# Layer 0 of a four-layer convolution kernel: its transfers divided anew among three queues, Wu in column tiles, an image's opening emitted in parts

## The chip, the cores and the metric

The kernel runs on one core of a Trainium2 chip. A core has TensorE (PE: matmuls; PEld is its loading of weights), VectorE (DVE), ScalarE (ACT), GpSimd (POOL) and SyncE (SP); transfers are issued from the queues of SP, ACT and POOL. The metric is device time in microseconds (us) of one execution, the median of several. The program is written with a tile layer that decides from the emitted code in which order each engine meets its instructions and where it waits.[...]

## The reference

The input is x with shape (32, 8, 256, 256) in float32. There are four layers, each x = x + f(groupnorm(x)); the change touches layer 0 alone.

```python
def _L0_conv_ref(x, K_local, Wp, bp, Wu, bu, Wg1, bg1, Wg2, bg2):
    R, EPS, BETA, STEPS = (3.9, 0.3, 0.15, 15)
    drive = x
    grid = drive
    for _ in range(STEPS):                                  # "the lattice"
        mapped = R * grid * (1.0 - grid)
        local = _conv(mapped, K_local, groups=8)            # 3x3, depthwise
        physics = (1.0 - EPS) * mapped + EPS * local
        grid = (1.0 - BETA) * physics + BETA * drive
    cml_out = jnp.clip(grid, 0.0001, 1.0 - 0.0001)
    h = jax.nn.relu(_conv(x, Wp, bp))                       # 3x3, 8 -> 128 channels
    nca_out = jax.nn.sigmoid(_conv(h, Wu, bu))              # 1x1, 128 -> 8
    gin = jnp.concatenate([x, cml_out, nca_out], axis=1)    # 24 channels
    g = jax.nn.sigmoid(_conv(jax.nn.relu(_conv(gin, Wg1, bg1)), Wg2, bg2))
    return g * cml_out + (1.0 - g) * nca_out

x = x + _L0_conv_ref(_gn(x), ...)    # _gn: 4 groups of 2 channels, mean and variance of each image
x = x + _L1_conv_ref(_gn(x), ...)    # quantised 3x3 convolution
x = x + _L2_conv_ref(_gn(x), ...)    # 3x3 convolution
x = x + _L3_conv_ref(_gn(x), ...)    # 5x5 depthwise convolution
```

## The kernel before

For each image two generators are interleaved: `lattice(b)` (load, sums, normalisation, 15 steps, result to DRAM) and `gated(b - 1)` (the hidden layer with Wp and Wu, then the gate). Each `yield` of the lattice says how much of its image is emitted, and the driver emits as much gated work beside it. The lattice of image b needs its own earlier steps; the gated work of image b - 1 needs only what lies in DRAM.

```python
def spread(half):                       # border points of neighbouring patches, 4 transfers
    ...
        nc.sync.dma_start(to[q : q + n * m, 0:long], window(state, at, dims))

def lattice(b):
    xi = xb[:, :, 1 : 1 + W]            # xb: one buffer for all images
    nc.gpsimd.dma_start(xi, x[b].rearrange("c (k r) w -> (c k) r w", k=HB))
    nc.gpsimd.dma_start(on_rows(xr_d[b % 3], W), x[b].rearrange(...))
    bn = small.tile([P, RB, 6], F32, name="bn0")
    for r in range(RB):
        nc.vector.bn_stats(bn[:, r, :], xb[:, r, 1 : 1 + W])
    group_stats(psum, bn, st, gavg_sb)  # two tiny matmuls (L94, L101), a square root on ACT
    yield 3
    ...                                 # flat (dr) and xb: normalised, on DVE
    nc.gpsimd.dma_start(window(xn_d[b % 3], ...), xb.rearrange("p r w -> p (r w)"))
    nc.gpsimd.dma_start(on_rows(nr_d[b % 3], WP), xb)
    yield 3
    for t4 in range(TX // 4):           # 32 transposes (L259), copied back by ACT
        ...
        if t4 % 4 == 3:
            yield 0.5
    for c in range(C):                  # first state, on DVE; spread after channels 3 and 7
        ...
    yield 1
    for step in range(STEPS):
        for half in range(2):           # "half-step": four channels
            for c in range(4 * half, 4 * half + 4):
                ps = ps_c.tile([P, 512], F32, name="psc")
                nc.tensor.matmul(o, patch_sb[:, c, :], v, start=True, stop=False)       # L281
                nc.tensor.matmul(o, ring_sb[:, c, :], rings[half]..., start=False, stop=True)  # L282
                nc.vector.scalar_tensor_tensor(v, o, FLOOR, dr[:, c], ALU.max, ALU.add)
                nc.vector.scalar_tensor_tensor(v, v, 1.0, v, ALU.subtract, ALU.mult)    # not in the last step
            spread(half)                # not in the last step
            yield 1
    for t4 in range(TX // 4):           # 32 transposes back (L302), copied to xb by DVE
        ...
    nc.gpsimd.dma_start(on_rows(cr_d[b % 3], WP), xb)

def gated(b):
    beside(nc.gpsimd, ha, nr, 0)        # rows beside each block, for the whole image
    beside(nc.gpsimd, ha, cr, 48)
    def hidden(r2):                     # two rows of every block, 16 rows of positions
        pn = ps_n.tile([P, 512], F32, name="psn")
        def second(hh, r):              # Wu in a 128-column weight, all columns but 8 zero
            nc.tensor.matmul(
                pn, wu_sb[:, C * (RB - 1 - r) : C * (RB - 1 - r) + P], hh,              # L344
                start=r == 0, stop=r == RB - 1,
            )
        for half in range(2):
            im = imp.tile([72, 2, 8 * WP], F32, name="im")      # two buffers
            ...nc.scalar.dma_start(im[...], window(xn, ...))    # 6 transfers
            for j in range(8):
                nc.tensor.matmul(ph, wp_sb, im[:, :, j * WP : j * WP + W], ...)         # L360
                nc.scalar.activation(hh, ph, AF.Relu, bias=bp_sb)
                if late is not None:
                    second(*late)
                late = (hh, 8 * half + j)
                yield
        second(*late)
        nc.scalar.activation(nh[:, 2 * r2 : 2 * r2 + 2, 1 : 1 + W], pn..., AF.Sigmoid, bias=bu_sb)
        beside_two(r2)                  # hb, from nh, on SP
    def gate(r2):
        ...                             # xq, cq, xc loaded on ACT
        for s, src in enumerate((xq, cq, nh[:, k0 : k0 + 2, :])):
            for dx in range(3):
                nc.tensor.matmul(o, wg1_sb[:, s, dx, :], src[:, :, dx : dx + W], ...)   # L393
            yield
        nc.tensor.matmul(o, wga_sb, ha[:, k0 : k0 + 2, 0:W], start=False, stop=False)   # L398
        nc.tensor.matmul(o, wgb_sb, hb[:, k0 : k0 + 2, 0:W], start=False, stop=True)    # L399
        nc.scalar.activation(g1, pg, AF.Relu, bias=bg1_sb)
        yield
        nc.tensor.matmul(pq, wg2_sb, g1, start=True, stop=True)                         # L404
        nc.scalar.activation(gt, pq, AF.Sigmoid, bias=bg2_sb)
        nc.gpsimd.tensor_tensor(df, ci, ni, ALU.subtract)
        nc.gpsimd.tensor_tensor(gt, gt, df, ALU.mult)
        nc.vector.tensor_tensor(gt, gt, ni, ALU.add)                                    # L413
        nc.vector.tensor_tensor(xc, xc, gt, ALU.add)                                    # L414
        ...                             # sums and extremes on DVE
        nc.gpsimd.dma_start(x1_d[b][:, bass.ts(r2, 512)], flat)
        yield
    for r2 in range(NCH + 1):           # NCH = 8
        if r2 < NCH:
            yield from hidden(r2)
        if r2 > 0:
            yield from gate(r2 - 1)

for b in range(B):
    at = 0
    for load in lattice(b):
        at += load
        due = ((b - 1.2) * LATTICE + at) * GATED / LATTICE
        while done < due:
            next(rest); done += 1
```

## Time and profile before

| | |
|---|---|
| time, median of 3 runs | 21,496.32 us (21,488.26 to 21,503.26) |
| span of the profiled execution | 21,491.9 us |
| mean granted TensorE clock | 0.948 |
| layer 0 (to its last Wu matmul) | 18,904 us |
| DVE busy | 38% |
| ACT busy | 19% |
| POOL busy | 7% |
| transfers | 2,307.92 MB, mean 107 GB/s |

How to read it: busy shares are averages over the whole span; where work waits is read from the timeline and from the stretches around one image. A row of a group gives line, engine, operation, tiles out<-in, shapes and count, then busy time in us, mean ns of one, and the engine's idle time before it with what ended it. Ends of matmuls are modelled, so their rate is read from start to start. The granted clock is the share of full speed at which TensorE was allowed to run.

### The profile page before, as it was taken

The page shows a single profiled execution, that of the slowest core. Times are in us where ns is not written, and L with a number is a line of the kernel's source. Part 1 is how long each engine was busy: PE and PEld are TensorE (multiplying, and loading weights), DVE is VectorE, ACT ScalarE, POOL GpSimd, SP SyncE. Part 2 cuts the span into 40 slices and gives each one's busy share as a digit, 9 for nine tenths or more (in the row PEclk, how much of TensorE's full clock was granted, in tenths as well). Part 3 has the DMA queues.
Part 4 walks back from the last instruction along what each step waited for, and adds up shares of the span by engine and source line. Part 5 has one row for each costly group of instructions (what it writes and reads, how often), then busy time and mean ns, then how long its engine had stood idle before and what let it go on. Part 6 is the DMA issues. An engine that isn't in the chain of part 4 may idle for free.

```text
span 21491.9 us, 137690 instructions
## 1 busy us (share of the span) xinstructions
PE 19778.0 (92%) x46664; PEld 8662.7 (40%) x46664; DVE 8103.2 (38%) x13657; ACT 4075.8 (19%) x5790; POOL 1570.3 (7%) x1649
## 2 busy tenths in 40 slices
PE   6899999999999999999999999999999999989999
PEld 2343443434343444444343434344443434434444
DVE  4333333333333333333333333333333333245554
ACT  0111222212212111222222212121122222211110
POOL 0000000000000000000000000000000000011111
PEclk8999999999999999999999999999999999999999
DMA  5444444444444444444444444444444444345554
GB/s 112 104 104 105 103 109 106 107 108 108 105 109 106 108 103 106 105 105 108 105 110 107 107 106 108 107 106 102 105 106 108 107 107 105 84 106 126 126 126 109
DMA packets 525150, 2307.92 MB, mean 107 GB/s; under 512 B 111468, under 2 KB 179540, under 8 KB 356388
## 3 DMA queue, kind: packets, MB, share of 16 engines
q1 hardware_dynamic: 213668, 835.31, 21.3%
q10 hardware_dynamic: 172032, 810.61, 13.3%
q0 software_dynamic: 138752, 653.18, 11.5%
q8 instruction: 377, 6.18, 0.1%
q14 instruction: 321, 2.63, 0.0%
HBM read 1129.33 MB, written 471.38 MB: 74 GB/s over the span
## 4 chain that ended last, share of the span: by engine, by line
PE 79%; issue 8%; DMA 7%; DVE 3%; POOL 1%; ACT 1%; SPq 0%; ACTq 0%; POOLq 0%; DVEq 0%
PE ph L360 15%; PE psn L344 15%; PE psc L282 14%; PE psc L281 14%; PE pg L393 7%; PE psv L578 5%; PE psv L499 4%; DMA rings<-state 2%; DMA hb<-nh 2%; DMA xb<-in_x 1%; PE psv L503 1%; PE pq L404 1%; PE psv L582 1%; PE pg L399 1%; PE pg L398 1%
## 5 line engine op out<-in xcount | busy, mean ns | idle before, releaser
L289 DVE SCALAR_TENSOR_TENSOR state<-psc,dr 128x512 f32<-128x512 f32 x3840 | 2620.8, 689 | 7462.1 <-PE psc L282 5203.8
L365 ACT ACTIVATE hh<-ph,bp_sb 128x512 f32<-128x512 f32 x4096 | 2812.6, 687 | 8527.0 <-PE ph L360 7196.7
L360 PE MATMUL ph<-im,wp_sb 72*128 72x512 f32 x8192 | 4301.8, 622 | 26.6 <-DMA im<-xn_d 14.1
L282 PE MATMUL psc<-rings,ring_sb 80*128 80x512 f32 x7680 | 4006.9, 607 | 325.5 <-issue 271.6
L344 PE MATMUL psn<-hh,wu_sb 128*128 128x512 f32 x8192 | 4255.1, 612 | 21.8 <-ACT hh L365 21.7
L281 PE MATMUL psc<-state,patch_sb 128*128 128x512 f32 x7680 | 3932.0, 597 | 117.5 <-DVE state L289 115.5
L360 PEld LDWEIGHTS ph<-im,wp_sb 72*128 72x128 f32 x8192 | 1614.7, 199 | 2063.1 <-issue 1449.1
L344 PEld LDWEIGHTS psn<-hh,wu_sb 128*128 128x128 f32 x8192 | 1565.4, 194 | 2182.1 <-issue 1841.7
L291 DVE SCALAR_TENSOR_TENSOR state<-state 128x512 f32<-128x512 f32 x3584 | 2387.4, 695 | 30.5
L282 PEld LDWEIGHTS psc<-rings,ring_sb 80*128 80x128 f32 x7680 | 1478.6, 194 | 2215.4 <-issue 2194.8
L281 PEld LDWEIGHTS psc<-state,patch_sb 128*128 128x128 f32 x7680 | 1448.5, 190 | 2047.9 <-issue 1696.9
L413 DVE TENSOR_TENSOR gt<-gt,nh 128x512 f32<-128x512 f32 x256 | 177.9, 695 | 3176.7 <-POOL gt L412 3176.7
L412 POOL TENSOR_TENSOR gt<-gt,df 128x512 f32<-128x512 f32 x256 | 328.9, 1285 | 12404.6 <-ACT gt L406 11178.1
L578 PE MATMUL psv<-xr,w_sb 128*128 128x512 f32 x2560 | 1159.9, 595 | 0.5 <-DVE xr L563 0.5
L401 ACT ACTIVATE g<-pg,bg_sb 128x512 f32<-128x512 f32 x256 | 176.3, 689 | 3642.6 <-PE pg L399 3185.5
L94 PE MATMUL ps<-mv,gavg_sb 128*128 128x1 f32 x64 | 17.8, 348 | 785.1 <-DVE mv L92 785.1
L393 PE MATMUL pg<-xq,wg_sb 128*128 128x512 f32 x1536 | 713.4, 596 | 0.0
L499 PE MATMUL psv<-xh,w_sb 128*128 128x512 f32 x1536 | 704.1, 595 | 8.1 <-DVE xh L535 4.1
L578 PEld LDWEIGHTS psv<-xr,w_sb 128*128 128x128 f32 x2560 | 475.5, 189 | 565.5 <-issue 561.1
L393 PE MATMUL pg<-nh,wg_sb 128*128 128x512 f32 x1536 | 701.2, 592 | 0.0
L393 PE MATMUL pg<-cq,wg_sb 128*128 128x512 f32 x1536 | 701.0, 592 | 0.0
L411 POOL TENSOR_TENSOR df<-cq,nh 128x512 f32<-128x512 f32 x256 | 436.6, 1706 | 2127.7 <-ACT nh L371 2021.2
(132 smaller groups left out, 9430.8 us busy)
## 6 DMA issues: line engine op xcount, KB each, us to landing
im<-xn_d ACTq DMA_DIRECT2D x3072, 193.3 KB
rings<-state SPq DMA_DIRECT2D x1920, 213.8 KB
rings<-state SPq DMA_DIRECT2D x1920, 142.5 KB
xn_d<-xb POOLq DMA_DIRECT2D x32, 2064.0 KB, 23.6
nr_d<-xb POOLq DMA_DIRECT2D x32, 2064.0 KB, 29.4
xq<-nr_d ACTq DMA_DIRECT2D x128, 516.0 KB
cr_d<-xb POOLq DMA_DIRECT2D x32, 2064.0 KB, 11.2
cq<-cr_d ACTq DMA_DIRECT2D x128, 516.0 KB
```

Of the source, the lines that this page charges most:

```text
L281: nc.tensor.matmul(o, patch_sb[:, c, :], v, start=True, stop=False)
L282: nc.tensor.matmul(o, ring_sb[:, c, :], rings[half][:, c % 4, 0 : TX * SY].rearrange("p (x y) -> p x y", y=SY)[:, :, 0:TY], start=False, s ...
L289: nc.vector.scalar_tensor_tensor(v, o, FLOOR, dr[:, c], ALU.max, ALU.add)
L291: nc.vector.scalar_tensor_tensor(v, v, 1.0, v, ALU.subtract, ALU.mult)
L344: nc.tensor.matmul(pn, wu_sb[:, C * (RB - 1 - r) : C * (RB - 1 - r) + P], hh, start=r == 0, stop=r == RB - 1,)
L360: nc.tensor.matmul(ph.rearrange("p (k w) -> p k w", w=W), wp_sb, im[:, :, j * WP : j * WP + W], start=True, stop=True,)
L365: nc.scalar.activation(hh, ph, AF.Relu, bias=bp_sb)
L393: nc.tensor.matmul(o, wg1_sb[:, s, dx, :], src[:, :, dx : dx + W], start=s == dx == 0, stop=False,)
L411: nc.gpsimd.tensor_tensor(df, ci, ni, ALU.subtract)
L412: nc.gpsimd.tensor_tensor(gt, gt, df, ALU.mult)
L499: nc.tensor.matmul(o, w[:, dx, :], src[:, 2 * i : 2 * i + 2, dx : dx + W], start=dx == 0, stop=False,)
L578: nc.tensor.matmul(o, w3_sb[:, dx, :], xr[:, k, 2 * g : 2 * g + 2, dx : dx + W], start=dx == 0, stop=False,)
```

## The change

It touches the emission and placement of layer 0, not what it computes.

- Transfers: an image's own large ones (xb, xr_d, xn_d, nr_d, cr_d) go from POOL's queue to SP's; the im loads from ACT's to POOL's; the rows beside a block (ha, hb) from POOL's and SP's to ACT's, per quarter of an image or per pair of blocks and in two buffers instead of one whole-image buffer.
- Wu: a weight of 32 columns that writes a quarter of the partitions of pn, with rows ordered so that successive matmuls alternate between two such quarters, four at a time.
- An image's load, sums and normalisation: a `yield` after the load, so that gated work is emitted between load and sums, and other weights for the later parts.
- The gate: one pair of blocks later than before, emitted within the hidden layer of a later pair.
- Two products of the gate go from POOL to DVE; pg takes its bank from another pool.

```diff
-            nc.gpsimd.dma_start(xi, x[b].rearrange("c (k r) w -> (c k) r w", k=HB))
-            nc.gpsimd.dma_start(
+            nc.sync.dma_start(xi, x[b].rearrange("c (k r) w -> (c k) r w", k=HB))
+            nc.sync.dma_start(
                 on_rows(xr_d[b % 3], W), x[b].rearrange("c (k r) w -> (c k) r w", k=HB)
             )
+            yield 6
...
             group_stats(psum, bn, st, gavg_sb)
-            yield 3
+            yield 2
...
-            nc.gpsimd.dma_start(
+            nc.sync.dma_start(
                 window(xn_d[b % 3], WP, [[HP * WP, C], [RB * WP, HB], [1, RB * WP]]),
                 xb.rearrange("p r w -> p (r w)"),
             )
-            nc.gpsimd.dma_start(on_rows(nr_d[b % 3], WP), xb)
+            nc.sync.dma_start(on_rows(nr_d[b % 3], WP), xb)
             yield 3
...
-            yield 1
+            yield 1.5
...
-            nc.gpsimd.dma_start(on_rows(cr_d[b % 3], WP), xb)
+            nc.sync.dma_start(on_rows(cr_d[b % 3], WP), xb)
...
-                def second(hh, r):
-                    nc.tensor.matmul(
-                        pn, wu_sb[:, C * (RB - 1 - r) : C * (RB - 1 - r) + P], hh,
-                        start=r == 0, stop=r == RB - 1,
-                    )
+                def second():
+                    for hh, r in late:
+                        q, i = divmod(r, 4)
+                        nc.tensor.matmul(
+                            pn[32 * q : 32 * q + 32, :], wu_sb[:, i, :], hh,
+                            start=i == 0, stop=i == 3,
+                        )
+                    late.clear()
...
-                            nc.scalar.dma_start(
+                            nc.gpsimd.dma_start(
                                 im[24 * dy : 24 * dy + 24, k, 0:run],
...
-                    for j in range(8):
...
+                    for rows in ((0, 4, 1, 5), (2, 6, 3, 7)):
+                        four = []
+                        for i, j in enumerate(rows):
...
+                            hh = hp.tile([P, 512], F32, name="hh", bufs=6)
+                            nc.scalar.activation(hh, ph, AF.Relu, bias=bp_sb)
+                            four.append((hh, 8 * half + j))
+                            if i == 1:
+                                second()
+                            yield
+                        late += four
+                second()
...
-                beside_two(r2)
+                if r2 > 0:
+                    beside_blocks(hbs[(r2 - 1) % 2], nh, 0, 2 * r2 - 2, 2, 1)
+                if r2 == NCH - 1:
+                    beside_blocks(hbs[r2 % 2], nh, 0, 2 * r2, 2, 1)
...
+                    quarter["ha"] = qp.tile([96, 4, WP], F32, name="ha")
+                    for q, t in ((0, nr), (48, cr)):
+                        beside_blocks(quarter["ha"], t, q, k0, 4, 0)      # on ACT's queue
...
-                pg = psum.tile([P, 512], F32, name="pg", tag="ps")
+                pg = ps_n.tile([P, 512], F32, name="pg", tag="pn")
...
-                nc.gpsimd.tensor_tensor(df, ci, ni, ALU.subtract)
-                nc.gpsimd.tensor_tensor(gt, gt, df, ALU.mult)
+                nc.vector.tensor_tensor(df, ci, ni, ALU.subtract)
+                nc.vector.tensor_tensor(gt, gt, df, ALU.mult)
...
-            for r2 in range(NCH + 1):
-                if r2 < NCH:
-                    yield from hidden(r2)
-                if r2 > 0:
-                    yield from gate(r2 - 1)
+            gates = (None for r2 in range(NCH) for _ in gate(r2))
+            for r2 in range(NCH):
+                for i, _ in enumerate(hidden(r2)):
+                    yield
+                    if r2 > 1 and i % 3 == 2:
+                        next(gates)
+                        yield
+            for _ in gates:
+                yield
...
-                due = ((b - 1.2) * LATTICE + at) * GATED / LATTICE
+                due = ((b - 1.25) * LATTICE + at) * GATED / LATTICE
...
-    wu = np.zeros((P, 2 * P - C), f)
-    wu[:, P - C : P] = inputs["L0_conv_Wu"][:, :, 0, 0].T
+    wu = np.zeros((P, 4, 4, C), f)
+    for r in range(4):
+        wu[:, r, r] = inputs["L0_conv_Wu"][:, :, 0, 0].T
```

## The prediction

> **What bounds the kernel now.** First the page: who is busy, at which clock, and what the chain that ended last is made of.
>
> ```profile
> span 21491.9 us, 137690 instructions
> PE 19778.0 (92%) x46664; PEld 8662.7 (40%) x46664; DVE 8103.2 (38%) x13657; ACT 4075.8 (19%) x5790; POOL 1570.3 (7%) x1649
> PE   6899999999999999999999999999999999989999
> PEclk8999999999999999999999999999999999999999
> PE 79%; issue 8%; DMA 7%; DVE 3%; POOL 1%; ACT 1%; SPq 0%; ACTq 0%; POOLq 0%; DVEq 0%
> PE ph L360 15%; PE psn L344 15%; PE psc L282 14%; PE psc L281 14%; PE pg L393 7%; PE psv L578 5%; PE psv L499 4%; DMA rings<-state 2%; DMA hb<-nh 2%; DMA xb<-in_x 1%; PE psv L503 1%; PE pq L404 1%; PE psv L582 1%; PE pg L399 1%; PE pg L398 1%
> ```
>
> TensorE bounds it: 92% busy and 79% of the chain, no other engine over 38%. Layer 0 (until the last Wu matmul at 18,904 us) is what changes. The transposes that open its second and its last image start at 430 and 17,985 us, thirty images apart, so an image costs **585 us**. The groups tell what a matmul costs:
>
> ```profile
> L360 PE MATMUL ph<-im,wp_sb 72*128 72x512 f32 x8192 | 4301.8, 622 | 26.6 <-DMA im<-xn_d 14.1
> L344 PE MATMUL psn<-hh,wu_sb 128*128 128x512 f32 x8192 | 4255.1, 612 | 21.8 <-ACT hh L365 21.7
> ```
>
> 4,096 matmuls of the program are 8,192 records: each f32 matmul runs as two passes. In a dense stretch of the timeline six passes start every 2.57 us (10,011.98, 10,014.55, 10,017.13), so a pass takes 0.429 us and a matmul 0.86 us, and its record lasts 0.59 us, 0.16 us longer. Per image, lines 281, 282, 344, 360, 393, 398, 399 and 404 have 37,888 / 32 = 1,184 passes, 508 us; 64 transposes at 0.13 us (eight in 1.03 us) add 8 us, the sums 2 us: **518 us of work in 585**. So 67 us an image are lost. The view by stretches finds where, in the image that opens near 9,700 us:
>
> ```profile
> 9700.00:9840.00 140.00, 100.20 (x225) 44.61 (x224) 37.59 (x77) 33.15 (x45) 16.71 (x17) 0.78 0.55 152
> 9840.00:10240.00 400.00, 398.84 (x922) 172.88 (x921) 154.53 (x236) 74.80 (x108) 15.82 (x13) 1.00 0.46 98
> ```
>
> (Columns: length, busy time and count of PE, PEld, DVE, ACT, POOL, granted clock, DMA share, GB/s.) The later 400 us are full at clock 1.00. The 140 us around the change of image hold 225 records, some 32 of them transposes: 193 × 0.429 + 32 × 0.13 = 87 us of work. **So about 53 of the 67 us are lost there.** The timeline of TensorE names the holes:
>
> ```profile
> 9702.58 2.12 PE L344 MATMUL psn<-hh,wu_sb 128*128 128x512 f32 x4
> 9728.29 0.56 PE L94 MATMUL ps<-mv,gavg_sb 128*128 128x1 f32 x2 [23.58 <-DVE mv L92]
> 9730.19 3.76 PE L360 MATMUL ph<-im,wp_sb 72*128 72x512 f32 x4
> 9749.59 1.10 PE L399 MATMUL pg<-hb,wgb_sb 72*128 72x512 f32 x2 [3.45 <-DMA hb<-nh]
> 9823.31 3.75 PE L282 MATMUL psc<-rings,ring_sb 80*128 80x512 f32 x4 [9.68 <-issue]
> ```
>
> The sums of the next image (L94) stand in TensorE's order only four matmuls after the last transposes; until cr_d is written, xb loaded and summed, it idles 23.6 us. Then 3.5 us for hb and 9.7 us for the first rings, and after each long hole passes start 0.85 us apart (four in 3.76 us), half speed.
>
> **What the Trainium skill says.** "TensorEngine Tiling (Array Packing)", Tiling Modes, Key Properties: tiles of the array run in parallel, and a change of tiling mode drains the engine. "TensorE: Matmul & The Clock Gate", Part 3 (Packing small matmuls): three column tiles of 32, N=512, gave 2.38×, and matmuls start and end in order. No run here shows either; the trace of before has no 128×32 tile in the loop. The same page, Part 1: after an idle window of some 3.4 us the clock falls to half, and returns after some 3.4 us of work. The trace agrees: clock 0.78 in the stretch with the holes. "DMA: Bandwidth & Descriptors", Issuing engines are not separate DMA queues: all queues share 16 engines and only issue time is saved. The trace agrees in so far as xn_d and nr_d, issued together, land after 23.6 and 29.4 us against 11.2 us for cr_d of the same size alone:
>
> ```profile
> xn_d<-xb POOLq DMA_DIRECT2D x32, 2064.0 KB, 23.6
> nr_d<-xb POOLq DMA_DIRECT2D x32, 2064.0 KB, 29.4
> cr_d<-xb POOLq DMA_DIRECT2D x32, 2064.0 KB, 11.2
> ```
>
> **Part 1: the opening of an image, +40 us.** In the changed program's order 28 full matmuls (18 ph, 9 pg, 1 pq) and 18 Wu matmuls stand between the last transpose and the sums: 28 × 0.86 + 18 × 0.6 (part 3) = 35 us. The load needs, from the timeline of before, 9,699.9 to 9,728.3 = 28 us. So the 23.6 us hole and its slow clock go. After the sums come 23 full and 8 Wu matmuls, 25 us, for the normalisation, and between the first state and the first rings matmuls 7 ph and 8 Wu, 11 us, against the 9.7 us hole. Gates one pair later, with hb's transfer a whole pair ahead: the 3.5 us go.
> Against it stands a new wait. The large transfers (cr_d, xb, xn_d, nr_d, xr_d) move to SP, and ha's loads to ACT; both share eight completion semaphores in turn, and by the program an ha load on ACT waits until xn_d has landed, another until nr_d has. If they still take 24 and 29 us from normalisation (some 9 us after the sums), nr_d lands 38 us after them, when TensorE's 25 us are over; ACT, which must also evacuate the transposes, is held. I take 13 us an image, slow clock included. 53 − 13 = 40.
>
> **Part 2: lattice steps alone, −20 us.** The order shows something that the diff does not: in the steady state the last 7 of an image's 30 half-steps have no gated work beside them (before, all 30 have). What such a half-step costs is seen in image 0 of before, which runs alone:
>
> ```profile
> 168.13 1.13 PE L281 MATMUL psc<-state,patch_sb 128*128 128x512 f32 x2 [1.13 <-DVE state L289]
> 173.91 2.81 PE L282 MATMUL psc<-rings,ring_sb 80*128 80x512 f32 x6 [0.93 <-DMA rings<-state]
> 177.74 1.13 PE L281 MATMUL psc<-state,patch_sb 128*128 128x512 f32 x2 [1.02 <-DVE state L289]
> ```
>
> 9.6 us from step to step, for 16 passes = 6.9 us. 7 × 2.7 = 19 us, with the edges 20. The clock stays at 1.00 there (stretch 200 to 300 us).
>
> **Part 3: Wu in column tiles, +20 us.** 128 Wu matmuls an image keep 512 columns and two passes; alone that saves nothing. Only overlap does. The order of rows alternates two column tiles. If passes start in order and a pass waits only for its own tile, a group of four (a a b b a' a' b' b') takes 5 slots instead of 8, a run of three 4 instead of 6, a single one 2. The changed order has, per image, 18 runs of four, 13 of three, 17 of one: 90 + 52 + 34 = 176 slots against 256, 80 × 0.429 = 34 us saved. A drain at each end of 48 runs, estimated at the 0.16 us by which a record outlasts its slot, costs 96 × 0.16 = 15 us. 34 − 15 = 19, say 20; that is 0.7 us a matmul against 0.86.
>
> **Part 4: the rest, 0.** Two 128x512 products per gate move from POOL (1.71 and 1.29 us) to DVE at about 0.69 us each; the addition behind them (L414, 1.34 us beside POOL, against 0.69 for L413) should fall to 0.7. DVE gains 0.7 us × 8 per image, at 27% busy: off the path. 96 im loads an image on POOL at about 0.6 us of issue are 58 us of 585: room enough, and ACT is rid of 96 × 0.65 us.
>
> **Sum.** 40 − 20 + 20 = 40 us an image, 545 instead of 585. Over 31 changes of image plus part 3 alone for the tail: about 1,270 us. Layers 1 to 3 (2,590 us) don't change. 21,496 − 1,270 ≈ **20,220 us**, −5.9%.
>
> **Rivals.** (a) The tiles don't overlap and only drain: Wu costs 15 us more than now instead of 20 less, 35 × 32 = 1,120 us worse: 21,300, "same". For it: no run here shows f32 tiles overlapping. Against: the program gives the passes distinct tiles. (b) They overlap with no drain to speak of: another 15 us, 19,750. (c) ACT's waits for xn_d and nr_d, or im loads that now compete on POOL's queue with 10 MB of the opening, hold TensorE as long as before: part 1 brings 10 us, 21,200. For it: DMA is 55% busy and 152 GB/s in that stretch already. Against: 35 us of work now lie there. (d) The scheduler's order fits and no new wait appears: 13 us more, 19,800. All in favour: 19,300.
>
> **Range and chances.** Half-widths of about 15 us an image for part 3, 15 for part 1, 8 for part 2 combine to some 22 us, 700 us in all; to the good side (b) and (d) may meet: 19,350 to 21,000. Slower needs (a) and (c) together. Faster by over 2% (below 21,066): 0.87; within: 0.08; slower: 0.05.
>
> **What would show it.** Part 1: no idle of 20 us before L94, clock near 1.00 throughout; wrong if L259's evacuation waits for xn_d or nr_d over 13 us. Part 2: 9.6 us steps before the L302 transposes. Part 3: starts of L351 records closer than 0.43 us on average; wrong if they are 0.43 us or more, with gaps at each change of tile.

## The result, and the profile after

The changed kernel takes **20,867 us** (median of 4 runs, 20,862.22 to 20,889.42), beside 21,494 us of the kernel before in the same session: ratio 0.971, 95% interval 0.9693 to 0.9727. That is 627 us less. The forecast was 1,276 us less, and half of it did not come.

The page of the changed kernel, the lines that answer to those of before:

```profile
span 20887.6 us, 135122 instructions
PE 19060.9 (91%) x46664; PEld 7483.3 (36%) x46664; DVE 8119.2 (39%) x14169; ACT 4058.6 (19%) x5790; POOL 2257.9 (11%) x3921
PEclk8999999999999999999999999999999999899999
PE 23%; DMA 2%; DVE 1%; ACT 0%; issue 0%; POOL 0%; SPq 0%; DVEq 0%; ACTq 0%; POOLq 0%
```

TensorE still bounds the kernel at 91%. The chain of work is of no use here: its shares add up to 26%, so it covers only the end of the program. The transposes that open images 1 and 31 start at 418 and 17,408 us: 566 us an image instead of 585, and 545 were forecast. The groups of TensorE show where to look (busy time, mean ns, idle time before them and what ended it):

```profile
L370 PE MATMUL ph<-im,wp_sb 72*128 72x512 f32 x8192 | 4232.4, 638 | 7.4 <-ACT hh L375 7.4
L351 PE MATMUL pn<-hh,wu_sb 128*32 128x512 f32 x8192 | 2545.6, 616 | 37.2 <-ACT hh L375 37.2
L417 PE MATMUL pg<-hb,wgb_sb 72*128 72x512 f32 x512 | 331.9, 735 | 859.1 <-DMA hb<-nh 845.4
```

Wu's 8,192 passes fell from 4,255 to 2,546 us. But L417, the matmul that reads hb, has 859 us of idle time in front of it, 845 of them waiting for hb's transfer. The forecast had that wait at zero. The timeline of TensorE around one change of image shows it (start, length, work, idle time before it):

```profile
9391.34 1.04 PE L351 MATMUL pn<-hh,wu_sb 128*32 128x512 f32 x2 [0.98 <-ACT hh L375]
9406.44 2.08 PE L417 MATMUL pg<-hb,wgb_sb 72*128 72x512 f32 x2 [14.06 <-DMA hb<-nh]
9408.31 10.45 PE L370 MATMUL ph<-im,wp_sb 72*128 72x512 f32 x12
...
9437.89 0.28 PE L94 MATMUL ps<-mv,gavg_sb 128*128 128x1 f32 x2
...
9453.11 2.84 PE L411 MATMUL pg<-xq,wg_sb 128*128 128x512 f32 x6 [0.78 <-ACT nh L382]
9467.91 2.04 PE L417 MATMUL pg<-hb,wgb_sb 72*128 72x512 f32 x2 [11.95 <-DMA hb<-nh]
```

Two things are to be seen. L94, which stood behind a hole of 23.6 us before, now has none: that part of the forecast came. In its place stand two holes of 14.1 and 12.0 us before L417, and twelve passes at half speed behind the first (10.45 us). The first L417 stands directly behind the last Wu matmul of the pair that fed its transfer; ACT issued hb at 9,393.14, 13 us before. Over images 4 to 27 the two are always the L417 of the sixth and of the seventh of an image's eight gates (15.0 and 12.0 us in the mean); the other six wait for no hb. The view by stretches of the same opening (length, busy time and count of PE, PEld, DVE, ACT, POOL, granted clock, DMA share, GB/s):

```profile
9370.00:9510.00 140.00, 106.65 (x273) 41.46 (x274) 42.46 (x88) 39.25 (x58) 18.99 (x34) 0.80 0.64 151
9390.00:9407.00 17.00, 1.97 (x4) 0.64 (x4) 2.92 (x5) 1.38 (x2) 5.02 (x9) 0.69 0.96 212
9446.00:9470.00 24.00, 11.27 (x25) 3.69 (x24) 4.69 (x8) 3.93 (x6) 2.25 (x4) 0.82 0.73 191
9510.00:9880.00 370.00, 364.90 (x889) 139.88 (x888) 137.57 (x220) 77.76 (x109) 39.00 (x70) 1.00 0.56 102
```

In the stretch of the first wait the transfer engines are nearly full (0.96, 212 GB/s), in that of the second they are not (0.73, 191 GB/s). The clock in the 140 us is 0.80, hardly above the 0.78 of before.

The next table adds up the starts of TensorE over images 4 to 27, in us per image. "Work" is start to start where nothing is waited for; a hole of over 0.25 us goes to its releaser; "slow clock" is what passes over 0.43 us cost where they start 0.75 us or more apart without a hole. The last three columns are versions from the experiments below.

| us per image | before | changed | e9 | e17 | e18 |
|---|---|---|---|---|---|
| image | 585.4 | 565.9 | 553.2 | 537.4 | 549.5 |
| work | 521.9 | 494.9 | 492.4 | 519.0 | 496.2 |
| of it Wu | 111.9 | 74.2 | 70.4 | 110.5 | 75.5 |
| all holes | 48.5 | 52.3 | 48.8 | 12.8 | 35.2 |
| hole: load and sums of the image (before L94) | 24.1 | 0 | 9.7 | 3.1 | 3.9 |
| hole: hb | 7.5 | 27.4 | 3.3 | 0 | 0 |
| hole: ACT (hh, g, gt, nh) | 3.1 | 4.2 | 13.9 | 7.2 | 7.8 |
| hole: the lattice itself (state, rings) | 3.0 | 14.2 | 15.6 | 1.1 | 18.9 |
| hole: first rings of an image | 9.2 | 0 | 0.8 | 0 | 0.4 |
| slow clock | 14.7 | 18.7 | 12.0 | 5.7 | 18.2 |

From before to changed: work −27, holes +3.8, slow clock +4.0, together −19.2 of the measured −19.5. **By this sum the whole net gain is TensorE's shorter work, and the holes only changed their names.** The sum doesn't say what each part of the change brings by itself; e4 and e6 below do. Why the hb holes came, whether they were all that was lost, and what the tiles are worth, is what the runs had to tell.

### The profile page after: what moved, and what is told of

It is laid out like the page before. It is cut to its first block, busy times and chain, and to the rows that moved or that the text cites. A ratio compares the mean times of both kernels' runs of the same rounds, so it can differ in the third digit from the quotient of the medians.

```text
span 20887.6 us, 135122 instructions
## 1 busy us (share of the span) xinstructions
PE 19060.9 (91%) x46664; PEld 7483.3 (36%) x46664; DVE 8119.2 (39%) x14169; ACT 4058.6 (19%) x5790; POOL 2257.9 (11%) x3921
## 5 line engine op out<-in xcount | busy, mean ns | idle before, releaser
L370 PE MATMUL ph<-im,wp_sb 72*128 72x512 f32 x8192 | 4232.4, 638 | 7.4 <-ACT hh L375 7.4
L281 PE MATMUL psc<-state,patch_sb 128*128 128x512 f32 x7680 | 3805.9, 615 | 342.1 <-DVE state L289 337.7
L282 PE MATMUL psc<-rings,ring_sb 80*128 80x512 f32 x7680 | 3719.9, 606 | 181.4 <-DMA rings<-state 170.1
L362 POOL DMA_DIRECT2D im<-xn_d x3072 | 1707.8, 560 | 13437.5 <-PE ph L370 12997.8
L351 PE MATMUL pn<-hh,wu_sb 128*32 128x512 f32 x8192 | 2545.6, 616 | 37.2 <-ACT hh L375 37.2
L351 PEld LDWEIGHTS pn<-hh,wu_sb 128*32 128x32 f32 x8192 | 455.2, 111 | 1867.1 <-issue 1767.2
L417 PE MATMUL pg<-hb,wgb_sb 72*128 72x512 f32 x512 | 331.9, 735 | 859.1 <-DMA hb<-nh 845.4
L430 DVE TENSOR_TENSOR gt<-gt,df 128x512 f32<-128x512 f32 x256 | 177.3, 693 | 2228.9 <-ACT gt L424 2228.9
L411 PE MATMUL pg<-cq,wg_sb 128*128 128x512 f32 x1536 | 789.0, 639 | 0.0
L411 PE MATMUL pg<-xq,wg_sb 128*128 128x512 f32 x1536 | 734.1, 603 | 47.5 <-ACT g L419 24.1
L552 ACT ACTIVATE x<-psv,b_sb,sc 128x512 f32<-128x512 f32 x256 | 183.9, 774 | 1750.8 <-PE psv L528 1749.7
```

What stands on the lines that cost most here:

```text
L282: nc.tensor.matmul(o, ring_sb[:, c, :], rings[half][:, c % 4, 0 : TX * SY].rearrange("p (x y) -> p x y", y=SY)[:, :, 0:TY], start=False, s ...
L351: nc.tensor.matmul(pn[32 * q : 32 * q + 32, :], wu_sb[:, i, :], hh, start=i == 0, stop=i == 3,)
L362: nc.gpsimd.dma_start(im[24 * dy : 24 * dy + 24, k, 0:run], window(xn, at, [[HP * WP, C], [1, 3], [1, run]]),)
L370: nc.tensor.matmul(ph.rearrange("p (k w) -> p k w", w=W), wp_sb, im[:, :, j * WP : j * WP + W], start=True, stop=True,)
L417: nc.tensor.matmul(o, wgb_sb, hbs[r2 % 2][:, :, 0:W], start=False, stop=True)
```

## The experiments

Each was timed in three rounds beside the kernel before. Ratios are to the kernel before.

### e1 to e4: the gate later, the quarters elsewhere, the tiles undone

**e1, the gate three pairs later.**

```diff
-                    if r2 > 1 and i % 3 == 2:
+                    if r2 > 2 and i % 3 == 2:
```

> The changed kernel with the gate two pairs of blocks later instead of one (it starts beside the fourth hidden pair). Theory H (the new wait is hb: a matmul that needs hb stands right behind the last Wu matmul, and hb lands 13 to 14 us after its issue because other transfers share the engines): in this order 9 or more gate matmuls stand ahead of the hb matmuls, so the idle before L417 falls from 27 us an image to 5 to 10 and the slow clock behind it with it: 20,150 to 20,400 us. Rival R (the transfers of the opening are the bound, and a wait that is taken away comes back at im, xq or ha): within 100 us of the changed kernel, 20,870.

Measured: 20,562 us, ratio 0.9571 (0.9555 to 0.9587). This lies between the two expectations. hb's holes fell from 27.4 to 18.4 us an image: that of the seventh gate went, that of the sixth stayed (16.6 to 21.9 us), and a hole of 9.5 us came back before L94. The remaining wait turned out to be one that this edit makes: with two buffers of hb, the last pair's hb goes into the buffer of the pair two before it, whose gate has still to run. That gate waits for the wrong transfer and reads another pair's border rows, so this run leaves the proper border rows out for one pair in eight. e9 mends it.

**e2, the loads xq, cq and ha issued from POOL instead of ACT**, so that nothing stands before hb in ACT's queue.

```diff
-                        nc.scalar.dma_start(quarter[name], t[:, k0 : k0 + 4, :])
+                        nc.gpsimd.dma_start(quarter[name], t[:, k0 : k0 + 4, :])
...
-                        beside_blocks(quarter["ha"], t, q, k0, 4, 0)
+                        beside_blocks(quarter["ha"], t, q, k0, 4, 0, nc.gpsimd)
```

> The changed kernel with the per-quarter loads xq, cq and ha issued from POOL instead of ACT, so that hb has ACT's queue nearly for itself; TensorE's order is the same but for a few places. Theory F (hb waits behind ha and cq on its own queue): the first of the two hb waits of an image, 14 us, falls to 4 or less, the second (12 us, nothing ahead of it on ACT's queue) stays: about 20,500 us. Theory S (it shares the DMA engines with xb, im, xn_d and nr_d, whatever queue it is on): both stay, 20,800 to 20,950 us.

Measured: 20,753 us, 0.9651 (0.9637 to 0.9666); hb's holes 20.3 us instead of 27.4. The first of the two fell from 15.0 to 8.4 us, the second stayed (11.6). So hb's place in ACT's queue is about half of the first wait and hardly a part of the second.

**e3, the rows of Wu in an order that does not alternate between tiles.**

```diff
-                    for rows in ((0, 4, 1, 5), (2, 6, 3, 7)):
+                    for rows in ((0, 1, 4, 5), (2, 3, 6, 7)):
```

> The changed kernel with the rows of a group in the order 0, 1, 4, 5 (two matmuls of one column tile, then two of the other) instead of 0, 4, 1, 5. If a matmul overlaps only a neighbour of another tile, four matmuls take three times two passes instead of twice two: 0.86 us more for each run of four, about 15 to 25 us an image, 21,300 to 21,600 us. Rival: the engine overlaps them in any order, or the gain of the tiles is not overlap at all but cheaper weights: 20,870 us, unchanged.

Measured: 20,854 us, 0.9699 (0.9684 to 0.9713), the same as the changed kernel. So the overlap does not need the alternation, as the change and the prediction took it to (see the last section).

**e4, Wu in 128 columns again, the rest as changed.**

```diff
-                            pn[32 * q : 32 * q + 32, :], wu_sb[:, i, :], hh,
-                            start=i == 0, stop=i == 3,
+                            pn, wu_sb[:, C * (RB - 1 - r) : C * (RB - 1 - r) + P], hh,
+                            start=r == 0, stop=r == RB - 1,
```

> The changed kernel with Wu as before: weights of 128 columns, one accumulation over all 16 rows, in the changed order of rows. It undoes the column tiles alone; the scheduler then spreads the gated work over all 30 half-steps again. Theory: Wu costs 110 us an image instead of 74 (+33 with the entries, +1,030 us), lattice steps beside nothing disappear (-14, -430 us), and part of the hb waits (-10, -300 us): 21,100 to 21,300 us. Rival (the opening brought the 627 us and the tiles little): 20,850 or less.

Measured: 20,584 us, 0.9571 (0.9557 to 0.9585): 284 us *faster* than with tiles, although TensorE has 25 us more work an image. The rest of the change, without the tiles, takes an image from 585.4 to 556.6 us. The holes of the two orders show the difference. With the cheaper Wu the scheduler's order has the gated work earlier: with tiles the last seven half-steps of an image are bare, in full width none is (the first 29 of 30 take 13.7 us or more). hb's holes are 14.5 us instead of 27.4, the lattice's own 0.8 instead of 14.2, slow clock 11.4 instead of 18.7.

### e5 to e8: what makes hb late, and the tiles alone

**e5, the writes of nr_d and xr_d moved** in quarters to POOL's queue beside lattice steps 1 to 8 (counted from 0); TensorE's order is unchanged.

```diff
+                q = step - 1
+                if 0 <= q < 4:
+                    nc.gpsimd.dma_start(window(nr_d[b % 3], ...), xb[:, 4 * q : 4 * q + 4, :])
+                q = step - 5
+                if 0 <= q < 4:
+                    nc.gpsimd.dma_start(window(xr_d[b % 3], ...), x[b]...[:, 4 * q : 4 * q + 4, :])
```

> The changed kernel, with one thing moved: the two whole-image writes that nobody needs before the next image (nr_d and the copy xr_d) leave SP's queue at the opening and go out in quarters from POOL's queue beside lattice steps 2 to 9, where the transfers' mean share is about 0.4. TensorE's order stays exactly that of the changed kernel. Theory S (hb lands late because its packets share the DMA engines with these large transfers): the second wait for hb (12 us) falls below 4, the first (14 us, beside the image's own load) to 7 to 10, so hb's waits go from 27 to about 10 us an image, some slow clock goes with them, 566 us an image become about 545, and the time 20,150 to 20,450 us. Rival F (hb is late by its place on ACT's queue, behind ha and cq, or by its own latency): the waits stay at 27 and the time at 20,800 to 20,900. Rival R (the quarters now hold up the rings of the lattice): hb's waits fall and waits for rings grow by as much, 20,650 to 20,900.

Measured: 20,795 us, 0.967 (0.9656 to 0.9685), only 73 us less. The two holes before L417 (L425 here) stayed, at 14.3 and 11.0 us in the mean instead of 15.0 and 12.0. One of them, with the stretch in which it lies:

```profile
8218.60 1.44 ACTq L337 DMA_DIRECT2D hb<-nh  x2
8232.86 2.08 PE L425 MATMUL pg<-hb,wgb_sb 72*128 72x512 f32 x2 [15.02 <-DMA hb<-nh]
8220.00:8233.00 13.00, 0.14 (x1) 0.14 (x1) 0.00 (x0) 0.00 (x0) 1.96 (x4) 0.50 1.08 219
```

So neither of the two copies was the cause, and Theory S was wrong in naming them. The transfer engines are as full as before (1.08, 219 GB/s): the image's own load (2 MB), seven im loads (0.19 MB each) and, in ACT's queue, loads of ha and cq remain beside hb's two transfers of 48 KB. Rival F (place in the queue, or hb's own latency) forecast these waits and nearly this time; e2 shows the queue's part for the first wait. Whether less of the remaining traffic would let hb land sooner was not tried, so what makes up the 11 to 13 us of landing stays open.

**e6, one part alone: the kernel before with Wu in column tiles** in groups of four. The diff to before is Wu's weight and matmul, the grouping of rows, five buffers of hh, and a tag of their own for g1 and gt. A group's Wu matmuls are emitted after the first hidden matmul of the next group, where the changed kernel has them after the second.

```diff
-                        hh = hp.tile([P, 512], F32, name="hh")
+                            hh = hp.tile([P, 512], F32, name="hh", bufs=5)
...
-                g1 = hp.tile([P, 512], F32, name="g1", tag="hh")
+                g1 = hp.tile([P, 512], F32, name="g1", tag="gt", bufs=2)
```

> One part alone: the kernel before, with only Wu in column tiles in groups of four (five buffers of hh, the gate's g1 and gt in two of their own); transfers, opening and gate are those of before. My sum gave this part 20 us an image (34 of the shorter runs less 15 of drains), which would be 21,494 - 31 x 20 = about 20,870. What the changed kernel's starts show (112 us of Wu become 74) gives 33 to 38 us an image, less about 10 for four or five half-steps that the scheduler then leaves without gated work: 25 to 30 us, 20,570 to 20,720. The rival that the tiles bring nothing net, as the full-width run suggested: above 21,200.

Measured: **21,843 us, 1.0157 (1.0142 to 1.0172): 1.6% slower than before**, 595.1 us an image instead of 585.4. The rival had said above 21,200; a loss nobody had forecast. Wu's time fell as it should, from 111.9 to 70.6 us an image. But the order now has four half-steps without gated work and one almost without, and they show what such a bare half-step can cost (the timeline of SP, DVE and TensorE):

```profile
8382.14 18.07 SPq L221 DMA_DIRECT2D rings<-state  x8
...
8398.35 2.74 PE L282 MATMUL psc<-rings,ring_sb 80*128 80x512 f32 x6
...
8407.18 1.29 DVE L289 SCALAR_TENSOR_TENSOR state<-psc,dr 128x512 f32<-128x512 f32 x2 [9.80 <-DMA rings<-state]
8407.93 2.07 PE L281 MATMUL psc<-state,patch_sb 128*128 128x512 f32 x2 [6.84 <-DVE state L289]
```

DVE may not write the state until the rings have been read out of it; it waits 9.8 us for that transfer, and TensorE waits 6.8 us behind DVE. This half-step took 15.7 us for 6.9 us of work; six im loads and those of xq and cq were issued in the 14 us up to 8,397.8. It is not the bare half-step as such that costs: the order of before has two of them in each image, with gated work directly ahead, and they take 6.9 us each without a wait. Over an image the lattice's own holes grew from 3 to 36 us and slow clock from 15 to 30: more than the tiles' 41.

**e7, full width, and the gates of the last two pairs carried into the next image; e8, the same with e5's moved writes.**

```diff
+            mine = gates_of()               # all eight gates, then the image's sums
             for r2 in range(NCH):
+                from_ = mine if r2 > 1 else left
+                if r2 == 0 and carried:
+                    from_ = carried.pop(0)  # what the image before has left
...
+            carried.append(mine)
```

> Wu in full width in the changed order, and the last two pairs' gates of an image emitted within the first two pairs of the next image instead of at the end, so that hb's matmul of the second wait falls behind two further runs of hidden work. If the wait for hb at the second place is what the image's end cost, one of two waits goes: 8 to 12 us an image off the full-width run's 20,584, thus 20,250 to 20,400. If the wait only passes to another instruction (the gate behind it, or a hole at the sums' small matmul), 20,500 to 20,650.

> The run before it (full width, gate carried over), and the two writes moved to POOL's queue beside the lattice steps; the order on TensorE is the same in both. By S the remaining wait for hb (about 12 us) halves and the opening's slow clock shrinks: 8 to 12 us an image below the run before it, 20,000 to 20,150. By F the two runs agree within 30 us.

Measured: 20,745 us, 0.9649 (0.9633 to 0.9665), and 20,689 us, 0.9622 (0.9608 to 0.9637). e7 is slower than e4, though hb's holes fell from 14.5 to 6.8 us: TensorE now waits 18.1 us an image for ACT's hh. The wait passed on, by more than was gained. e8 gains 56 us on e7, no more than e5 gained.

### e9 to e12: hb really a pair ahead

**e9, the gate three pairs later with three buffers of hb.**

```diff
-        hbs = [wt.tile([72, 2, WP], F32, name=f"hb{i}") for i in range(2)]
+        hbs = [wt.tile([72, 2, WP], F32, name=f"hb{i}") for i in range(3)]
...                                        # and (NCH * b + r2) % 3 for r2 % 2
-                    if r2 > 1 and i % 3 == 2:
+                    if r2 > 2 and i % 3 == 2:
```

> The gate three pairs later, as in the first run, and three buffers of hb instead of two. With two, hb of an image's last pair went into the buffer of the pair two before it, whose gate had still to run, and that gate waited for it (16.6 us, the one wait for hb left there; its border rows were then those of another pair). With three, every gate's hb has been issued a whole pair ahead, which is what the prediction took for granted. If that step failed only because hb was asked for as soon as it was issued, hb's 18 us an image go, with some slow clock: 556 us an image become 533 to 540, and the time 19,900 to 20,100 us, which is within reach of the 545 us an image that was predicted for the change. If the opening is bound by its transfers whatever the gate does, the wait passes to im or to the sums' small matmul, and the time stays at 20,350 to 20,560.

Measured: 20,472 us, 0.9524 (0.9509 to 0.9538). hb's holes fell to 3.3 us (all at the seventh gate), so the step of the forecast is now nearly true, but the time fell by only 89 us from e1, and an image by 12.7 us from the changed kernel. The timeline of POOL, ACT and TensorE shows what stepped in:

```profile
8150.44 0.59 POOL L437 DMA_DIRECT2D x_d<-xc  x1 [35.97 <-DVE xc L432]
...
8167.15 0.33 ACTq L403 DMA_DIRECT2D xc<-xr_d  x1
8167.53 0.69 ACT L419 ACTIVATE g<-pg,bg_sb 128x512 f32<-128x512 f32 x1 [14.90 <-DMA x_d<-xc]
8168.27 2.07 PE L422 MATMUL pq<-g,wg_sb 128*128 128x512 f32 x2 [9.68 <-ACT g L419]
```

In ACT's program order the load of xc stands ahead of g, and it may not overwrite its buffer until the store x_d of an earlier pair has landed. That store was issued at 8,150.44 and landed after some 17 us, beside the writes of xn_d and nr_d. So ACT stood, g came 14.9 us late, and TensorE waited for g.

**e10, e9 in full width** (the edit of e4).

> The run before it with Wu in 128 columns. TensorE has 26 to 34 us more work an image, and the order has no half-step without gated work. In the changed kernel full width was 9 us an image faster than tiles, 13 of them hb's waits and 13 the lattice's own waits in its bare half-steps. If hb's waits are gone in both, the bare half-steps remain: tiles and full width come within 150 us of each other, full width at 20,000 to 20,200. If the tiles' saving is real and only hb's waits hid it, full width is slower than the run before it by 300 us or more.

Measured: 20,803 us, 0.967 (0.9656 to 0.9685). Here the tiles win, by 330 us, as the second expectation had it; the holes of full width are 23.5 us for ACT's g and 7.3 before L94.

**e11, full width, three buffers of hb, and the gate always three pairs behind, also across the border of an image.**

```diff
             for r2 in range(NCH):
+                old = carried.pop(0) if len(carried) == 3 else None
                 for i, _ in enumerate(hidden(r2)):
                     yield
-                    if r2 > 1 and i % 3 == 2:
-                        next(gates)
+                    if old is not None and i % 3 == 2:
+                        next(old)
                         yield
...
+                carried.append(gate(r2) if r2 < NCH - 1 else last())
```

> Full width, three buffers of hb, the gate always three pairs behind, across the border of an image too, so that no run of gates stands at an image's end; the order has no bare half-step, and both of hb's matmuls in the opening stand a pair or more behind their transfers. Expected 20,000 to 20,200, as the run before it; if the hidden layer in the opening then waits for ACT (18 us an image in the run with two pairs carried), 20,500 to 20,700.

Measured: 20,222 us, 0.9407 (0.9392 to 0.9423): no hole for hb, 11.8 us for ACT's hh.

**e12, e10 with 1.15 for 1.25 in the driver.**

> The full-width run with the gate three later and three buffers of hb, and the gated work emitted a tenth of an image nearer to its lattice (1.15 for 1.25), by which the end of an image's gates comes ahead of the sums instead of behind them. If the order inside the opening matters little, within 60 us of the full-width run with 1.25. If the sums' small matmul (a hole of 9 us in the first run) is what remains of the opening's loss, it is filled here and the time falls by a further 150 to 280 us.

Measured: 20,625 us, 0.9594 (0.958 to 0.9609); the hole of the load's sums is gone, 11.1 + 7.7 us for ACT's hh and g are there, and 7.6 us for the sums at an image's end.

### e13 to e18: ACT's queue

**e13, e9 with four buffers of xc instead of two; e14, the carried gate of e11 with four, in tiles; e15, the same in full width.**

```diff
-                xc = hp.tile([P, 2, W], F32, name="xc", bufs=2)
+                xc = hp.tile([P, 2, W], F32, name="xc", bufs=4)
```

> The run with the gate three later and three buffers of hb, with one number more: four buffers of xc instead of two; TensorE's order is the same. There ACT stood 11.9, 7.5 and 7.4 us at the load of xc, which waits until the store x_d of the pair two before has landed, and TensorE waited 14 us an image behind ACT's g. With four buffers the load waits for a store two pairs older. If that is what took the place of hb's wait, 12 to 17 us an image go: 20,472 becomes 19,950 to 20,120. If ACT's queue only passes the wait to its next load (xq, cq, ha), 20,330 to 20,470.

> The changed kernel (Wu in column tiles) with all that the runs pointed at: gate three pairs behind across the border of an image, three buffers of hb, four of xc. The opening then has no run of gates and no wait for hb or for ACT; what stays are eight bare half-steps (10 + 5 us of waits for the lattice itself) and the hole at the sums' small matmul (6 to 10 us). 492 us of work and 35 of waits and slow clock: 525 to 535 us an image, 19,650 to 19,950 us. If the opening is bound by its transfers anyway: 20,200 to 20,450.

> The same with Wu in full width, no bare half-step: 520 us of work and 12 to 18 of waits and slow clock, 531 to 538 us an image, 19,770 to 19,980 us; beside the run before it this says what the tiles are worth once the waits are out of the way (forecast: 0 to 150 us for the tiles). If ACT's queue holds the hidden layer at another load, it stays at 20,150 to 20,250.

Measured: 20,483 us, 0.9529 (0.9515 to 0.9543); 20,610 us, 0.9584 (0.9568 to 0.96); 20,205 us, 0.9401 (0.9387 to 0.9415). More buffers did nothing, and e14 lies above both of its expectations, with 28.4 us an image for ACT's hh. In ACT's program order the loads had moved two pairs forward, as far as the buffers allowed, and stood at the same place behind the same stores (issue to landing 18.6, 15.1 and 7.6 us in e13's trace). The buffer count did not help a load that the scheduler issues as early as the buffers permit, on the queue of an engine that also has work to do.

**e16, e9 with the load of xc issued from SP; e17, e11 with it (full width); e18, e17 in tiles.**

```diff
-                nc.scalar.dma_start(xc, xr[:, k0 : k0 + 2, :])
+                nc.sync.dma_start(xc, xr[:, k0 : k0 + 2, :])
```

> The gate three later with three buffers of hb, and the load of xc issued from SP's queue instead of ACT's; TensorE's order is that of the run with three buffers (20,472 us). Four buffers of xc did nothing, because the loads only moved two places forward in ACT's order, to wait for the same stores. If ACT's queue standing at that load is the cause of the 14 us of waits for ACT's g, they go now, with 2 to 4 us of slow clock: 19,950 to 20,130 us. If SP's own traffic is held by the load in turn (the writes of xn_d, the rings), or the wait passes to another load in ACT's queue, 20,300 to 20,480.

> The fastest so far (full width, gate always three pairs behind, three buffers of hb, 20,222 us) with xc's load on SP. The wait of the hidden layer for ACT's hh at the 81st us of an image (11 us) goes: 19,830 to 19,980 us; if another load takes its place, 20,150 to 20,250.

> The same in column tiles. The waits for ACT's hh (29 us an image in the run with four buffers) go, and with them some slow clock; seven or eight bare half-steps stay with 15 us of the lattice's own waits: 523 to 533 us an image, 19,560 to 19,900 us. If the tiles' time still goes into waits elsewhere (rings, xn_d, im), 20,200 to 20,600, and full width stays the faster form in every arrangement tried.

Measured: e16 20,361 us, 0.9469 (0.9454 to 0.9483). The wait for g fell to 1 us, but 11.1 us for ACT's gt came at the image's end, where ACT stands between a load of ha and gt; with e9's order of TensorE this took most of the gain. What held ACT there was not settled. e18 20,333 us, 0.9449 (0.9431 to 0.9467). **e17 19,971 us, 0.9289 (0.9275 to 0.9303), the fastest version: 4.3% below the changed kernel.** Its page, and its opening and rest of an image by stretches:

```profile
PE 19331.1 (97%) x46664; PEld 8570.1 (43%) x46664; DVE 8078.6 (40%) x14169; ACT 4021.2 (20%) x5790; POOL 2266.3 (11%) x3922
PEclk8999999999999999999999999999999999999999
7866.00:7976.00 110.00, 101.22 (x272) 47.36 (x273) 35.34 (x67) 38.86 (x60) 18.00 (x33) 0.94 0.65 154
7976.00:8370.00 394.00, 393.01 (x917) 172.67 (x916) 160.69 (x268) 76.13 (x107) 40.19 (x72) 1.00 0.59 110
```

TensorE is 97% busy, and the clock in the opening is 0.94 where it was 0.80. From the last transposes of an image to the next one's first lattice matmul it takes 107 us instead of 126, at the same rate of transfers (154 against 151 GB/s). So the opening was not bound by its transfers as such, only by the places at which someone waited for one. The wait for ACT's hh fell by about 4 us an image from e11 and did not go, and TensorE's order is another than in e11; so what the moved load brings by itself is seen in e16 alone (111 us at one order).

**What the tiles are worth** can be read from four pairs that differ in source only by Wu's form: tiles against full width 20,867 and 20,584 (changed, e4), 20,472 and 20,803 (e9, e10), 20,610 and 20,205 (e14, e15), 20,333 and 19,971 (e18, e17). The scheduler makes another order in each, so these are not tests of the tiles at one order. From e17 to e18 work falls by 22.8 us an image, holes rise by 22.4 (17.8 of them the lattice's own, with eight bare half-steps of 8.3 to 19.3 us) and slow clock by 12.5. Taken singly, the tiles cost 9.7 us an image (e6) and the rest brings 28.8 (e4), together 19.1; the changed kernel has 19.5. That the sums nearly agree proves little, as the holes lie elsewhere in each order.

## Why the prediction was wrong

The direction was right and the size was not: 40 us an image were forecast, 19.5 came. By its steps:

- **Part 1, the opening, +40: this failed, and at one sentence: "Gates one pair later, with hb's transfer a whole pair ahead: the 3.5 us go."** For the first five of an image's eight gates hb lands in time; the sixth and the seventh wait, and the eighth, whose hb is issued together with the seventh's, has nothing left to wait for. In TensorE's order the L417 of those two stands behind the Wu run whose results hb carries, with at most three matmuls between. For the seventh the source already has it so: the last hidden pair ends, hb of the last two pairs is issued, and the gates that are left follow without hidden work between. For the sixth the source has most of a pair between, and the scheduler put it otherwise. So hb's holes went from 7.5 to 27.4 us instead of to zero. The slow clock that was to go with the holes ("clock near 1.00 throughout") stayed: 14.4 us outside the bare half-steps, 14.7 before. The other two holes went as forecast: L94 24.1 to 0, first rings 9.2 to 0. With 3.5 us for the sums at an image's end (L456), part 1 brought about 10 us (24.1 + 9.2 − 19.9 − 3.5), not 40. e9 and e11 confirm the step's cause by undoing it (hb 3.3 and 0 us). They don't give back its price: in e9 other waits, ACT's g and the sums of the load, took 24 us. And e4 shows that about half of hb's 27.4 us comes only with the tiles (14.5 without).
- **The new wait that the prediction did put there, 13 us of ACT behind xn_d and nr_d**, was not seen in the changed kernel. Its kind was right, its place wrong: once hb was out of the way, ACT did stand for 14 us, at xc's load behind the store of x_d.
- **Part 2, bare half-steps, −20: this came as forecast.** Over images 4 to 27 the seven bare half-steps take 9.8 us each in the mean (8.3 to 11.6), against 6.9 us of passes: 20.3 us an image. The table's row for the lattice rose by 11 us only, because it holds nothing but waits; of the 20.3 us, 13.7 are waits, 4.3 slow clock and 2.2 passes set a little wider. That before "all 30 have" gated work is not quite so (two have none, at 6.9 us each), and e6 shows that 9.6 us is no constant: there such a step took 16 us.
- **Part 3, the tiles, +20**: mis-sized to the bad side. A run of four takes 1.84 us, 4.3 slots and not 5, and a run of three 1.83. The timeline of the changed kernel shows both, by the start of what follows:

```profile
9443.78 1.91 PE L351 MATMUL pn<-hh,wu_sb 128*32 128x512 f32 x8
9445.62 1.13 PE L370 MATMUL ph<-im,wp_sb 72*128 72x512 f32 x2
...
9448.40 1.90 PE L351 MATMUL pn<-hh,wu_sb 128*32 128x512 f32 x6
9450.23 1.13 PE L416 MATMUL pg<-ha,wga_sb 96*128 96x512 f32 x2
```

  18 × 1.84 + 13 × 1.83 + 17 × 0.98 = 74 us, which is the Wu row of the table, with the change of tile at a run's end in it; at its start 0.09 us lie on the matmul before. The slots so saved are the 34 us of the forecast; the drains that were to cost 15 us hardly cost anything beyond it, some 4 us at the starts (48 × 0.09). Outside the bare half-steps the work fell by 29 us in all. But the step also took the tiles for free of consequences in the order, while part 2 booked the bare half-steps without asking what made them. The pairs above say that they belong together.
- **Part 4, 0**, was not contradicted: no hole in the table is put down to the two products on DVE or to the issue of im on POOL. It was not tested by itself. The 27% given for DVE hold for the opening (37.59 of 140 us); from 1,594 to 18,003 us it is 36%.
- **The sum**: 10 − 20 + 29 = 19 us an image, and 19.5 were measured. (In the forecast 31 × 40 + 20 is 1,260 and not 1,270, which changes nothing.)
- **The rivals**: (c), 21,200 us, was nearest of them in number and in idea (a transfer that holds TensorE), and its 10 us for part 1 are what came, but it named the wrong transfers. (a) is refuted by the 1.84 us; (b), tiles with hardly a drain, is largely what came. The time lies inside the range by luck: part 1 missed by 30 us, twice its half-width of 15, and part 3 gave 9 of them back.

## What to carry to other kernels

When a producer's result goes through a transfer to the same engine, "one stage later" in the source is not a distance: read in the engine's program order what lies between the instruction that feeds the transfer and the one that waits for it, and set that against the landing time in the busiest stretch (13 us here, for two transfers of 48 KB). Look first at the last items of a loop, behind which the source has no later work. A load in the queue of an engine that also evacuates results can hold the evacuation for as long as its buffer is not free: here more buffers only moved it forward (e13), while another engine's queue took 111 us off at the same order (e16). And a cheaper operation changes a scheduler's order: judge it by the holes of the new order as well as by its own time.

## What the runs showed of the hardware that was not expected

- **Matmuls of two column tiles overlap out of program order.** In e3 the four matmuls of a run stand in the order a a b b (two tiles, two passes each). If they started in order, one tile's four passes would lie 0.43 us apart and only then the other's, some 3 us in all. The eight starts are at 0, 14, 454, 467, ... ns and the run takes 1.85 us, as with a b a b (0, 7, 453, 460, ...). Two matmuls of one tile alone start their passes at 0, 453, 882 and 1,311 ns. (The records don't name the tile; which pass belongs to which is read from the source's order and these starts.) Read so, TensorE starts a later matmul of a free tile before an earlier one of a busy tile. The Trainium skill ("TensorE: Matmul & The Clock Gate", Part 3, Packing small matmuls) says that matmuls start and end strictly in order; for starts, this trace differs.
- **A change between tiles and full width costs about 0.09 us at the start of a run and 0.10 at its end.** The start-to-start time from a matmul of the hidden layer to a first Wu pass is 521 ns against 429 within a kind; and the last pair of a run of four starts at 1,312 ns, the next full-width pass at 1,841, 529 ns later. The skill ("TensorEngine Tiling (Array Packing)", Tiling Modes, Key Properties) says that a change of mode drains the engine, without a figure.
- **Four Wu matmuls take 1.84 us in column tiles and 3.43 us in full width** (e4, eight starts), f32 with its two passes.
- **A store of 256 KB from POOL lands after 18.6 us** beside the writes of an image and after 7.6 us 30 us later (e13); a load that waits for such a store inherits the difference.
